# Attention and experts on one core: the low part of the probabilities in tiles of its own, multiplied after the high part

## The chip, the cores and the metric

The kernel runs on one core of one Trainium2 chip. The metric is the device time of one execution in microseconds (us), the median of several runs; lower is better.

## The reference

One transformer block on a sequence of 2048 tokens of width 256, batch 1. Attention has 16 heads of width 128; its weights come as codes times scales of blocks of 32 rows. Then a mixture of 8 experts with hidden width 176, of which each token uses two. Both halves have layer norms before and after, and a residual sum.

```python
q = layernorm(x) @ (wq_codes * repeat(wq_scales, 32)) + bq       # k, v alike
scores = einsum("bqhd,bkhd->bhqk", q, k) / sqrt(128)
attn = softmax(scores, axis=-1)
out = einsum("bhqk,bkhd->bqhd", attn, v).reshape(1, 2048, 2048)
x = x + layernorm(out @ (wo_codes * repeat(wo_scales, 32)) + bo)
y = layernorm(x)
combine = top2_of_softmax(y @ Wr), renormalised, spread over the 8 experts
h = silu(y @ Wg[e]) * (y @ Wu[e])
x = x + layernorm(sum over e of combine[e] * (h @ Wd[e]))
```

Everything is wanted to about float32 precision. TensorE multiplies 16-bit operands here, so the kernel splits each float32 operand into a 16-bit "high part" and the 16-bit rest, the "low part", and adds three products: high by high, high by low, low by high.

## The kernel before, in words

The time goes to attention, from about 30 to 1600 us of the span. Its work is a loop over 256 query tiles of 128 rows (16 tiles for each of 16 heads) plus two passes that only finish (loop variable g; t is the tile's number within the head). Each engine executes its own instructions in the order in which the program emits them: the kernel is written under a manual schedule, so that order is the order of the statements in this loop.

For one query tile:

- `scores_half`, twice: TensorE makes scores of 128 queries by 1024 keys in 6 matmuls of 512 columns (lines 486, 487, 490) in one of three PSUM buffers with the tag "s"; VectorE takes the row maximum (line 491).
- `softmax`: ScalarE takes the exponential of both halves (line 502) into a float32 tile p.
- One tile later: `high_part` (line 516) has ScalarE write the normalised high part ph (float16, three buffers), and SyncE issues a DMA transpose of it (line 519), since the product with the values wants the keys on the partitions. `low_half` (line 531) has VectorE write the low part pl (two buffers) in two halves, the first at the end of that tile, the second at the start of the tile after; behind the second SyncE issues the transpose of pl (line 535).

So SyncE's queue alternates: low part of tile k-2, high part of tile k-1, and so on, 512 transposes in all. Four query tiles make a block. Before the change, both parts of a block's four tiles go to one tile `PT[(h, block)]` of shape 128 x 4 x 32 x 128 (32 KB a partition): in the third dimension 0 to 15 is the high part and 16 to 31 the low part. The pool has two buffers, so the first transpose of block n+2 needs block n's tile to be free: all of its readers must be done.

The product with the values, `pv_part`, works on one block: 16 chunks of 128 keys, three matmuls of 512 columns each, 48 in all, into one PSUM bank ("pv"):

```python
nc.tensor.matmul(ps, vh, d[:, :, c, :], start=(c == 0), stop=False)        # L550
nc.tensor.matmul(ps, vh, d[:, :, 16 + c, :], start=False, stop=False)      # L551
nc.tensor.matmul(ps, vl, d[:, :, c, :], start=False, stop=(c == 15))       # L552
```

vh and vl are the parts of the values, from tiles `V[(pair, group)]` that hold two heads and 512 keys (four a pair of heads, pool tag "v" with seven buffers, which also serves the output weights and tiles of the last stage). The 48 matmuls are cut into 8 units of 6 (`pv_unit`), two units a query tile: unit 2g between the two halves of the scores of tile g and unit 2g+1 behind them. A lag of 13 units (`PVLAG`) puts unit 0 of block n in the second half of tile 4n+6 and unit 7 in the first half of tile 4n+10. The last transpose of block n's high part is issued in tile 4n+4, of its low part in tile 4n+5; the first of block n+2's high part in tile 4n+9.

Between these, `fill` puts the projections of the next Q, K and V (lines 224 and 249), which ScalarE copies out (237, 268) and GpSimd splits; GpSimd also loads and scales weights, and writes each block's attention output to HBM (`ot_d`, line 566).

In the last head, and behind it, the same queues also load the weights of the output projection and of the experts, and reload the attention output in pieces `oi` (`load_oi`, line 682). The last block's units (8 of them, `UEND+1` to `UEND+8`) stand behind the output projection of the first 512 tokens (`op_pass(0, ...)`, line 809), before the router of those tokens (`tr`, `router_a`, `router_b`) and the output projection of the next 512 (`op_mm(1, half, parts)`: a part takes 16 matmuls of 256 columns and reads one piece oi). The expert loop follows (`gate_up`, `down`).

Of the kernel before, what the change touches and what calls it, by code (L numbers as in the profile page):

```python
# [21 lines left out]
D = 256  # L22
# [15 lines left out]
def sandwich(  # L38
# [51 lines left out]
    crow = const.tile([128, D], F32)  # L90
# [4 lines left out]
    def tail_consts(i):  # L95
        if i == 0:
            nc.sync.dma_start(out=crow, in_=bo.partition_broadcast(128))
# [144 lines left out]
    def proj_v(p, t0, n, tag="pj", wide=None):  # L242
# [11 lines left out]
        if t0 % 4 == 0:  # L254
            V[(p, t0 // 4)] = kqv.tile([128, 2, 4, 256], HP, name="v", bufs=7)
# [222 lines left out]
    PT = {}  # L478
# [35 lines left out]
    def high_part(h, t, m, p):  # L514
        ph = soft.tile([128, S], HP, name="ph", bufs=3)
        nc.scalar.activation(ph, p, AF.Copy, scale=m[:, 6:7])  # L516
        if t % 4 == 0:
            PT[(h, t // 4)] = pt.tile([128, 4, 32, 128], HP, name="pt")
        nc.sync.dma_start_transpose(
            out=PT[(h, t // 4)][:, t % 4, 0:16, :], in_=ph  # L520
# [5 lines left out]
    def low_half(half, h, t, m, p, ph):  # L526
# [7 lines left out]
        if half == 1:  # L534
            nc.sync.dma_start_transpose(
                out=PT[(h, t // 4)][:, t % 4, 16:32, :], in_=LOW.pop((h, t))
            )
# [3 lines left out]
    def pv_part(h, b, c0, c1):  # L541
        d = PT[(h, b)]
        if c0 == 0:
            pvps[(h, b)] = psA.tile([128, 512], F32, name="pv")
        ps = pvps[(h, b)]
        dc = bass.ts(h % 2, 128)
        for c in range(c0, c1):
            v = V[(h // 2, c // 4)]
            vh, vl = v[:, 0, c % 4, dc], v[:, 1, c % 4, dc]
            nc.tensor.matmul(ps, vh, d[:, :, c, :], start=(c == 0), stop=False)  # L550
            nc.tensor.matmul(ps, vh, d[:, :, 16 + c, :], start=False, stop=False)  # L551
            nc.tensor.matmul(ps, vl, d[:, :, c, :], start=False, stop=(c == 15))  # L552
        if c1 == 16:
            if (h, b) == (NH - 1, 3):
                o = kqv.tile([128, 2, 512], HP, name="o_last", tag="v", bufs=7)
# [33 lines left out]
    def pv_unit(u):  # L589
        n, e = divmod(u - PVLAG, 8)  # L590
        if 0 <= n < 4 * NH:
            pv_part(n // 4, n % 4, 2 * e, 2 * e + 2)
# [36 lines left out]
    def dequant_wo(j):  # L629
        sc, cd = wo_raw.pop(j)  # L630
        if j % 4 == 0:
            wo.append(kqv.tile([128, 8, D], BF, name="wo", tag="v", bufs=7))
# [45 lines left out]
    def load_oi(b, half, j, tag="kT"):  # L678
        oi = kqv.tile(
            [128, 4, 2, 256], HP, name="oi", tag=tag, bufs={"kT": 8, "v": 7}[tag]  # L680
# [10 lines left out]
    gw = None  # L691
# [5 lines left out]
    def late(t):  # L697
        nonlocal gw
# [159 lines left out]
    def tr(b, kc, tag="pj"):  # L858
        xn = AT[b]
        if kc == 0 and b == 0:  # L860
            XT[b] = [
                kqv.tile([128, 2, 512], F32R, name="xT0", tag="v", bufs=7)
# [14 lines left out]
    def router_a(b, tag="pj"):  # L877
# [9 lines left out]
        if b == 0:  # L887
            LGT[b] = kqv.tile([8, 512], F32, name="lgT0", tag="v", bufs=7)
# [122 lines left out]
    def fin0(b):  # L1011
        y = kqv.tile([128, 4, D], F32, name="y", tag="v", bufs=7)
# [22 lines left out]
    def fin_last(b):  # L1035
        y = kqv.tile([128, 4, D], F32, name="y", tag="v", bufs=7)
# [42 lines left out]
    pv_unit(UEND + 4)  # L1079
    pv_unit(UEND + 5)  # L1080
# [12 lines left out]
    op_mm(1, 0, (0,), "s")  # L1093
# [18 lines left out]
    def load_x1(b):  # L1112
        X1[b] = tl.tile([128, 4, D], F32, name=f"x1_{b}")
# [4 lines left out]
    op_mm(1, 0, (1, 2), "s")  # L1118
# [6 lines left out]
    op_mm(1, 0, (3,), "s")  # L1125
# [99 lines left out]
```

## Time and profile before

| | |
|---|---|
| median of 3 runs | 1871.5 us (1870.53 to 1875.38) |
| the profiled execution | 1870.9 us, of which the span is 1869.1 us |
| TensorE matmul busy | 1785.9 us (96%), 8890 matmuls |
| VectorE busy | 1628.8 us (87%) |
| ScalarE busy | 1366.5 us (73%) |
| GpSimd busy | 937.8 us (50%) |
| DMA: queue 1 (SyncE's, transposes included) | 309.74 MB, 90.4% of 16 engines' span |
| transposes of the high and of the low part | 256 each, median 5.0 us from issue to landing |

How to read it: PE is TensorE's matmuls, PEld its weight loads, which run beside matmuls; DVE is VectorE, ACT ScalarE, POOL GpSimd, SP SyncE. "SPq" is SyncE's queue: the time that it needs to issue a DMA. L551 is line 551. A group is named by what it writes and reads, `pv<-pt,v`; behind "idle before" or in square brackets stands how long the engine was idle ahead of it and what ended that. In a list of waits the three numbers are the sum in us, how often, and the longest. In a timeline a row begins with its start and its length in us.

### The profile page before, as it was taken

To read this page: it belongs to the slowest core of one execution; us is meant where nothing else is said; L and a number is where in the kernel's file an instruction comes from. 1 tells how busy PE (TensorE), PEld (TensorE's weight loads), DVE (VectorE), ACT (ScalarE), POOL (GpSimd) and SP (SyncE) were. 2 spreads that over 40 slices of the span, in tenths; PEclk is the share of its full clock that TensorE was granted. 3 is DMA by queue.
4 is the path that set the end of the run, shared out by engine and by line. 5 is a ranking of instruction groups with operands and counts; after the bars stand their busy time and mean duration, and the time that the engine had idled before them with its cause. 6 is when DMAs were issued, how large, how long until landed. Compare 5 with 4: busy or idle time off the path is not lost. (4 is left out here: it accounts for less than half of the span.)

```text
span 1869.1 us, 25550 instructions
## 1 busy us (share of the span) xinstructions
PE 1785.9 (96%) x8890; PEld 933.7 (50%) x8890; DVE 1628.8 (87%) x2267; ACT 1366.5 (73%) x1730; POOL 937.8 (50%) x929
## 2 busy tenths in 40 slices
PE   7899999999999999999999999999999988999997
PEld 4344444444444444444444444444444334678886
DVE  7999998999898999999999999999999986457566
ACT  5888887888787888888888888887888775123232
POOL 2366565555655565556555656465446442233232
PEclk9999999999999999999999999999999999999999
DMA  2999999999999999999999999999999999982121
GB/s 84 176 199 198 195 200 191 186 199 197 195 186 187 194 197 200 195 197 193 200 197 193 198 199 201 195 192 197 192 187 207 215 221 227 268 222 69 52 75 51
DMA packets 1132529, 342.31 MB, mean 183 GB/s; under 512 B 1071232, under 2 KB 1119568, under 8 KB 1132400
## 3 DMA queue, kind: packets, MB, share of 16 engines
q1 hardware_dynamic: 1119712, 309.74, 90.4%
q0 software_dynamic: 10544, 29.40, 5.7%
q10 hardware_dynamic: 2144, 1.54, 0.3%
q8 instruction: 70, 1.15, 0.2%
q14 instruction: 59, 0.48, 0.1%
HBM read 53.22 MB, written 18.94 MB: 39 GB/s over the span
## 5 line engine op out<-in xcount | busy, mean ns | idle before, releaser
L531 DVE SCALAR_TENSOR_TENSOR pl<-p,m,ph 128x1024 f16<-128x1024 f32 x512 | 723.6, 1414 | 34.5 <-DMA pt<-pl 32.6
L502 ACT ACTIVATE p<-s,m,ssc 128x1024 f32<-128x1024 f32 x512 | 612.3, 1200 | 191.9 <-DVE m L495 175.8
L491 DVE TENSOR_REDUCE m<-s 128x1 f32<-128x1024 f32 x512 | 622.7, 1216 | 43.8 <-PE s L490 41.5
L516 ACT ACTIVATE ph<-p,m 128x2048 f16<-128x2048 f32 x256 | 512.8, 2003 | 79.1 <-ACT t L237 26.7
L551 PE MATMUL pv<-pt,v 128*128 128x512 f16 x1024 | 390.4, 381 | 38.8 <-DMA pt<-pl 38.5
L486 PE MATMUL s<-kT,qT 128*128 128x512 f16 x1024 | 389.7, 381 | 7.3 <-ACT p L502 6.6
L550 PE MATMUL pv<-pt,v 128*128 128x512 f16 x1024 | 390.4, 381 | 3.0 <-DMA pt<-ph 1.7
L552 PE MATMUL pv<-pt,v 128*128 128x512 f16 x1024 | 390.5, 381 | 0.0
L487 PE MATMUL s<-kT,qT 128*128 128x512 f16 x1024 | 389.6, 380 | 0.0
L490 PE MATMUL s<-kT,qT 128*128 128x512 f16 x1024 | 305.5, 380 | 0.0
L238 POOL CAST qT<-t 128x512 f16<-128x512 f32 x63 | 81.8, 1299 | 241.8 <-ACT t L237 241.8
L269 POOL CAST v<-t 128x256 f16<-128x256 f32 (+1 forms) x105 | 45.9, 437 | 285.7 <-ACT t L268 285.7
L551 PEld LDWEIGHTS <-v 128*128 128x128 f16 x1024 | 100.5, 98 | 169.0 <-issue 48.1
L550 PEld LDWEIGHTS <-v 128*128 128x128 f16 x1024 | 100.6, 98 | 126.3 <-issue 4.8
L552 PEld LDWEIGHTS <-v 128*128 128x128 f16 x1024 | 100.6, 98 | 121.7 <-issue 6.1
L490 PEld LDWEIGHTS <-qT 128*128 128x128 f16 x1024 | 100.4, 98 | 121.8 <-issue 1.6
L270 POOL TENSOR_TENSOR v<-t,v 128x256 f16<-128x256 f32 (+1 forms) x105 | 156.9, 1494 | 8.5
L487 PEld LDWEIGHTS <-qT 128*128 128x128 f16 x1024 | 100.5, 98 | 120.3 <-issue 14.5
L486 PEld LDWEIGHTS <-qT 128*128 128x128 f16 x1024 | 100.5, 98 | 110.4 <-issue 1.9
L978 POOL TENSOR_TENSOR hh<-sg,hh 128x512 fp32r<-128x512 f32 x42 | 54.5, 1298 | 143.5 <-ACT hh L977 106.2
L977 ACT CAST hh<-sg 128x512 fp32r<-128x512 f32 (+1 forms) x45 | 27.5, 611 | 117.2 <-DVE sg L989 117.2
L239 POOL TENSOR_TENSOR kT<-t,kT 128x512 f16<-128x512 f32 x60 | 97.7, 1628 | 5.1
(186 smaller groups left out, 2063.4 us busy)
## 6 DMA issues: line engine op xcount, KB each, us to landing
oi<-ot_d SPq DMA_DIRECT2D x32, 512.0 KB, 6.1
ot_d<-o POOLq DMA_DIRECT2D x63, 256.0 KB, 4.4
pt<-ph SPq DMA_TRANSPOSE x256, 5.0
pt<-pl SPq DMA_TRANSPOSE x256, 5.0
cu<-ct_d SPq DMA_DIRECT2D x16, 256.0 KB, 3.7
xt<-in_L_attn_x SPq DMA_DIRECT2D x4, 512.0 KB, 4.6
x<-in_L_attn_x SPq DMA_DIRECT2D x4, 512.0 KB, 6.0
st_s<-in_L_attn_wv_scales POOLq DMA_DIRECT2D x28, 64.0 KB, 4.2
```

The lines of the kernel that those rows point to most:

```text
L239: nc.gpsimd.tensor_tensor(t[:, 1, :], t32, t[:, 0, :], ALU.subtract)
L270: nc.gpsimd.tensor_tensor(v[:, 1, sl, :], t32, v[:, 0, sl, :], ALU.subtract)
L486: nc.tensor.matmul(s[:, j, :], q[:, 0, qc], k[:, 0, :], start=True, stop=False)
L487: nc.tensor.matmul(s[:, j, :], q[:, 0, qc], k[:, 1, :], start=False, stop=False)
L490: nc.tensor.matmul(s[:, j, :], q[:, 1, qc], k[:, 0, :], start=False, stop=True)
L491: nc.vector.tensor_reduce(m[:, half : half + 1], s, AX.XY, ALU.max)
L502: nc.scalar.activation(p[:, bass.ts(i, 1024)], s, AF.Exp, bias=m[:, 2:3], scale=ssc[:, 0:1], accum_out=m[:, 3 + i : 4 + i],)
L516: nc.scalar.activation(ph, p, AF.Copy, scale=m[:, 6:7])
L531: nc.vector.scalar_tensor_tensor(pl[:, cs], p[:, cs], m[:, 6:7], ph[:, cs], ALU.mult, ALU.subtract)
L550: nc.tensor.matmul(ps, vh, d[:, :, c, :], start=(c == 0), stop=False)
L551: nc.tensor.matmul(ps, vh, d[:, :, 16 + c, :], start=False, stop=False)
L552: nc.tensor.matmul(ps, vl, d[:, :, c, :], start=False, stop=(c == 15))
```

## The change

- The transposed parts get tiles of their own: `pth` for the high part and `ptl` for the low part, each 128 x 4 x 16 x 128 with two buffers (the same memory in all).
- The 48 products of a block are reordered: first, chunk by chunk, high probabilities by high and by low values (32 matmuls), then high values by low probabilities (16). Cut into 8 units of 6 as before: units 0 to 4 and a third of unit 5 read `pth`, the rest reads `ptl`.
- The tag "v" has eight buffers instead of seven. To make room, `crow` (the output bias row) is loaded in the last head instead of the first, into memory that is free by then, and the residual tile `x1_1` takes a buffer with the tag "v".
- Behind the loop, parts 0 and 1 of `op_mm(1, 0)` move ahead of the last block's unit 4; parts 2 and 3 follow at the places shown.

```diff
-            PT[(h, t // 4)] = pt.tile([128, 4, 32, 128], HP, name="pt")
+            PT[(h, t // 4)] = pt.tile([128, 4, 16, 128], HP, name="pth")
         nc.sync.dma_start_transpose(
-            out=PT[(h, t // 4)][:, t % 4, 0:16, :], in_=ph
+            out=PT[(h, t // 4)][:, t % 4], in_=ph
         )
...
         if half == 1:
+            if t % 4 == 0:
+                PTL[(h, t // 4)] = pt.tile([128, 4, 16, 128], HP, name="ptl")
             nc.sync.dma_start_transpose(
-                out=PT[(h, t // 4)][:, t % 4, 16:32, :], in_=LOW.pop((h, t))
+                out=PTL[(h, t // 4)][:, t % 4], in_=LOW.pop((h, t))
             )
...
+    PV_ORDER = [(c, i) for c in range(16) for i in (0, 1)]
+    PV_ORDER += [(c, 2) for c in range(16)]
+
-    def pv_part(h, b, c0, c1):
-        d = PT[(h, b)]
-        if c0 == 0:
+    def pv_part(h, b, e):
+        if e == 0:
             pvps[(h, b)] = psA.tile([128, 512], F32, name="pv")
...
-        for c in range(c0, c1):
-            v = V[(h // 2, c // 4)]
-            vh, vl = v[:, 0, c % 4, dc], v[:, 1, c % 4, dc]
-            nc.tensor.matmul(ps, vh, d[:, :, c, :], start=(c == 0), stop=False)
-            nc.tensor.matmul(ps, vh, d[:, :, 16 + c, :], start=False, stop=False)
-            nc.tensor.matmul(ps, vl, d[:, :, c, :], start=False, stop=(c == 15))
-        if c1 == 16:
+        for n in range(6 * e, 6 * e + 6):
+            c, i = PV_ORDER[n]
+            d = (PTL if i == 2 else PT)[(h, b)]
+            nc.tensor.matmul(
+                ps, V[(h // 2, c // 4)][:, i % 2, c % 4, dc], d[:, :, c, :],
+                start=(n == 0), stop=(n == 47),
+            )
+        if e == 7:
...
             gw = rp.tile([128, 2, 2, EI], F32R)
+            crow = rp.tile([128, D], F32)
+            nc.sync.dma_start(out=crow, in_=bo.partition_broadcast(128))
...
     pv_unit(UEND + 4)
+    op_mm(1, 0, (0, 1), "s")
     pv_unit(UEND + 5)
...
     router_a(0, "s")
-    op_mm(1, 0, (0,), "s")
+    op_mm(1, 0, (2,), "s")
     router_b(0, "s")
...
+        if b == 1:
+            X1[b] = kqv.tile([128, 4, D], F32, name="x1_1", tag="v", bufs=8)
+        else:
+            X1[b] = tl.tile([128, 4, D], F32, name=f"x1_{b}")
...
-    op_mm(1, 0, (1, 2), "s")
+    op_mm(1, 0, (3,), "s")
     router_d(0)
...
-    op_mm(1, 0, (3,), "s")
```

More of the change, by code (lines that the diff above doesn't have):

```diff
@@ L89, in sandwich @@
     bv3 = const.tile([128, NH, 3], BF)
-    crow = const.tile([128, D], F32)
     rst = const.tile([128, 2, E], F32)
@@ L96, in tail_consts @@
         if i == 0:
-            nc.sync.dma_start(out=crow, in_=bo.partition_broadcast(128))
             nc.sync.dma_start(out=rst, in_=wr.rearrange("(kc p) e -> p kc e", p=128))
@@ L254, in proj_v @@
         if t0 % 4 == 0:
-            V[(p, t0 // 4)] = kqv.tile([128, 2, 4, 256], HP, name="v", bufs=7)
+            V[(p, t0 // 4)] = kqv.tile([128, 2, 4, 256], HP, name="v", bufs=8)
         v = V[(p, t0 // 4)]
@@ L475, in sandwich @@
     soft = soft_ctx.enter_context(tc.tile_pool(name="soft", bufs=2, reuse_waits="tile"))
-    PT = {}
+    PT, PTL = {}, {}
     def scores_half(h, t, half, m):
@@ L546, in pv_part @@
         dc = bass.ts(h % 2, 128)
-        for c in range(c0, c1):
-            v = V[(h // 2, c // 4)]
-            vh, vl = v[:, 0, c % 4, dc], v[:, 1, c % 4, dc]
-            nc.tensor.matmul(ps, vh, d[:, :, c, :], start=(c == 0), stop=False)
-            nc.tensor.matmul(ps, vh, d[:, :, 16 + c, :], start=False, stop=False)
-            nc.tensor.matmul(ps, vl, d[:, :, c, :], start=False, stop=(c == 15))
-        if c1 == 16:
+        for n in range(6 * e, 6 * e + 6):
[6 more added lines that the diff above has]
+        if e == 7:
             if (h, b) == (NH - 1, 3):
-                o = kqv.tile([128, 2, 512], HP, name="o_last", tag="v", bufs=7)
+                o = kqv.tile([128, 2, 512], HP, name="o_last", tag="v", bufs=8)
                 nc.scalar.activation(o[:, 0, :], ps, AF.Copy, scale=1.0 / PS)
@@ L591, in pv_unit @@
         if 0 <= n < 4 * NH:
-            pv_part(n // 4, n % 4, 2 * e, 2 * e + 2)
+            pv_part(n // 4, n % 4, e)
     wo = []
@@ L631, in dequant_wo @@
         if j % 4 == 0:
-            wo.append(kqv.tile([128, 8, D], BF, name="wo", tag="v", bufs=7))
+            wo.append(kqv.tile([128, 8, D], BF, name="wo", tag="v", bufs=8))
         hs = slice(2 * (j % 4), 2 * (j % 4) + 2)
@@ L679, in load_oi @@
         oi = kqv.tile(
-            [128, 4, 2, 256], HP, name="oi", tag=tag, bufs={"kT": 8, "v": 7}[tag]
+            [128, 4, 2, 256], HP, name="oi", tag=tag, bufs={"kT": 8, "v": 8}[tag]
         )
@@ L690, in sandwich @@
     prev = None
-    gw = None
+    gw, crow = None, None
     gst = {}
@@ L697, in late @@
     def late(t):
-        nonlocal gw
+        nonlocal gw, crow
         if t in WO_LOAD:
@@ L861, in tr @@
             XT[b] = [
-                kqv.tile([128, 2, 512], F32R, name="xT0", tag="v", bufs=7)
+                kqv.tile([128, 2, 512], F32R, name="xT0", tag="v", bufs=8)
                 for _ in range(2)
@@ L887, in router_a @@
         if b == 0:
-            LGT[b] = kqv.tile([8, 512], F32, name="lgT0", tag="v", bufs=7)
+            LGT[b] = kqv.tile([8, 512], F32, name="lgT0", tag="v", bufs=8)
         else:
@@ L1011, in fin0 @@
     def fin0(b):
-        y = kqv.tile([128, 4, D], F32, name="y", tag="v", bufs=7)
+        y = kqv.tile([128, 4, D], F32, name="y", tag="v", bufs=8)
         nc.scalar.copy(y, DPS.pop(b)[1])
@@ L1035, in fin_last @@
     def fin_last(b):
-        y = kqv.tile([128, 4, D], F32, name="y", tag="v", bufs=7)
+        y = kqv.tile([128, 4, D], F32, name="y", tag="v", bufs=8)
         mv = small.tile([128, 4, 2], F32, name="mv3")
@@ L1112, in load_x1 @@
     def load_x1(b):
-        X1[b] = tl.tile([128, 4, D], F32, name=f"x1_{b}")
+        if b == 1:
+            X1[b] = kqv.tile([128, 4, D], F32, name="x1_1", tag="v", bufs=8)
+        else:
+            X1[b] = tl.tile([128, 4, D], F32, name=f"x1_{b}")
         nc.sync.dma_start(out=X1[b], in_=XV[:, b])
```

## The prediction, made before the changed kernel ran

> **What bounds the kernel now.** I read the busy times first, then TensorE's waits by stage, then single blocks in the order of time, then the waits of the engines around them. All idle times below are of heads 1 to 14 (127 to 1467 us from the start) unless said otherwise.
>
> The stages (columns: stretch, length, then busy us and count of PE, PEld, DVE, ACT, POOL, then granted clock, DMA share, GB/s):
>
> ```profile
> 127.00:1467.00 1340.00, 1314.10 (x6258) 610.55 (x6256) 1251.99 (x1568) 1118.84 (x1390) 761.90 (x765) 1.00 1.08 196
> 1467.00:1600.00 133.00, 114.97 (x576) 56.51 (x574) 98.79 (x132) 85.08 (x101) 42.16 (x34) 0.96 1.12 225
> 1600.00:1642.00 42.00, 38.52 (x245) 27.63 (x245) 22.71 (x61) 9.65 (x15) 16.06 (x11) 0.96 1.04 279
> ```
>
> TensorE has 26 us of idle time in 1340, VectorE 88, and the DMA engines are never free on average. TensorE's waits in heads 1 to 14, then those of head 15 and after:
>
> ```profile
> PE pv L551 <- DMA pt<-pl: 23.3, 22, 2.6
> PE s L486 <- ACT p L502: 1.6, 2, 1.2
> ...
> PE pv L551 <- DMA pt<-pl: 14.2, 5, 4.2
> PE s L486 <- ACT p L502: 4.1, 3, 3.0
> PE pv L550 <- DMA pt<-ph: 1.7, 2, 1.2
> ```
>
> One wait is nearly all: line 551, the product with the low part, for the transpose of that low part. In one block:
>
> ```profile
> 889.04 0.38 PE L550 MATMUL pv<-pt,v 128*128 128x512 f16 x1
> ...
> 890.63 0.38 PE L551 MATMUL pv<-pt,v 128*128 128x512 f16 x1 [1.21 <-DMA pt<-pl]
> 890.84 0.38 PE L552 MATMUL pv<-pt,v 128*128 128x512 f16 x1
> ```
>
> The high product starts; the second instruction of the block stands 1.21 us. In a stream, starts lie 0.215 apart (0.21 to 0.22 by these lines) but each is shown 0.38 long, so a listed wait is about 0.165 too short: 23.3 + 22 x 0.165 = 26.9 us.
>
> From the starts of the first score matmul of each query tile I worked out the tile times of heads 1 to 14: nearly all are 6.04 (a tile with a Q or K projection) or 5.62 us (with a V projection), which is TensorE's own work: 24 matmuls x 0.2155 = 5.17, plus 4 x 0.2155 or 4 x 0.109. A head of such tiles is 93.3 us (91.5 for head 14); the real mean is (1467.4 - 127.1) / 14 = 95.7. The excess is 36.2 us over 14 heads, and 31.6 of it lies in tiles 2, 6, 10 and 14, the ones in whose second half a block of products begins; 3.1 in the tile after, mostly half-clock matmuls behind a long wait. So TensorE sets the pace, and it loses 34.7 us where a block begins.
>
> Why the low part is late: SyncE issues all transposes, and the first one of block n+2 waits for the last product of block n, which frees the shared tile.
>
> ```profile
> SPq L519 <- PE pv L552: 45.5, 41, 2.4
> ...
> DVE m L491 <- PE s L490: 32.6, 58, 2.5
> ...
> DVE pl L531 <- DMA pt<-pl: 13.8, 18, 1.8
> ```
>
> SyncE loses 45.5 us there (about 1.1 per hold), and its 447 transposes last 1214.7 us by their own durations (2.72 each), so it is over 90% taken and doesn't catch up quickly.
>
> **The Trainium skill.** "TensorE: Matmul & The Clock Gate", section "Back-to-back issue gap", gives N / 2.4 + 2.5 ns, 215.8 for 512 columns: the trace agrees (0.215 to 0.216). The same page, "What's actually happening", says that the array falls to half clock after an idle window of about 3.4 us: the trace agrees, behind the waits of 4.15 and 3.85 us at 1569 and 1602 matmuls start 0.43 apart for some us. "DMA: Bandwidth & Descriptors", "Anatomy of one DMA", says that a semaphore wait is served on the issuing sequencer before dispatch, so one held transpose holds all behind it: the 45.5 us above agree. The same page, "Issuing engines are not separate DMA queues", says that all issuers share 16 engines: the DMA share of 1.08 agrees.
>
> **The change, part by part.**
> Same work: still 48 matmuls and 48 weight loads a block. Weights now alternate high, low for 32 of them; each load takes 98 ns with or without a new weight before (lines 550 to 552 all show 98) under a 215 ns matmul: nothing. If that cover went, 48 x 98 ns a block, but no row shows a bare load. The 4 KB instead of 8 KB stride between query tiles of the moving operand is not shown by any row; I take 0 and keep 1 us a head as its bound either way.
>
> *First low product.* It moves from unit 0 to unit 5 of a block, 2.5 tiles (14.6 us) later. The worst wait is 4.2, so all of them go in the loop: 34.7 us with the half-clock share. High parts are still due at unit 0. The last one of a block is issued just ahead of the third low one and lands 5.0 us later: in the block shown issued at 882.48, due at 889.04, 1.5 us spare, in the block 72 us earlier 3.9. No wait of line 550 stands in heads 1 to 14. But what SyncE lacks over several blocks is no longer made good by waits for low parts, so I take 2 us of waits for high parts (bounds 0 and 12).
>
> *The held transpose.* High tiles are read in units 0 to 5 only, so the buffer is free one tile before its next transpose is issued; the hold of 45.5 us ends. The new hold, of the first low transpose of a block, is for unit 7 of block n: TensorE runs that within 1.3 us after the tile's first scores, while VectorE needs a 1.22 reduce, two small steps and a 1.4 low step after the same scores. The wait is over before the transpose is ready: 0. Behind it on SyncE would stand the next high transpose.
>
> *What is late next.* VectorE. Its idle time is 88.0, 32.6 of it for TensorE's scores; the rest, 55.4, is for ScalarE, for buffers of low parts and small gaps. A loop shorter by 34.7 leaves it 53.3, less than the 55.4. So it becomes an equal of TensorE, and the waits don't fall together: I take back a quarter, 9 us (bounds 2 and 25), as TensorE waiting at line 486 for score buffers. Loop: -34.7 + 2 + 9 = -23.7.
>
> *Head 15.* From 1451 to 1601 SyncE is taken without a break (62 DMAs, 142.7 us of issue in 150, no gap over 0.43): transposes with loads of weights and attention outputs between them. No held transpose is among them, so this stretch keeps its length, whatever TensorE gains. crow's load moves into it from head 0, where it cost nothing and saves nothing: one more issue, +0.5 by the neighbours (0.53).
>
> *Behind the last transpose:*
>
> ```profile
> 1596.32 3.64 SPq L535 DMA_TRANSPOSE pt<-pl  x1
> 1597.81 0.39 PE L550 MATMUL pv<-pt,v 128*128 128x512 f16 x1 [0.57 <-DMA pt<-ph]
> 1601.23 5.10 SPq L682 DMA_DIRECT2D oi<-ot_d  x4
> 1602.05 0.61 PE L551 MATMUL pv<-pt,v 128*128 128x512 f16 x1 [3.85 <-DMA pt<-pl]
> ```
>
> Now four units of high products run at once (4 x 1.29, to 1603.0), then 32 output matmuls (3.5), then the low ones. But those 32 read loads that SyncE issues at 1601.2 and 1601.8, behind the last transpose; the second lands at 1608.5. So 4.0 of wait and 1.7 of half clock (3.4 us at half) are exchanged for about 4 of another wait; the gain is some 2 us (bounds: a loss of 4, a gain of 6). The pass now holds one of three score buffers from there on; two are left to the two transposes and the router, which need each other's results anyway: 0.
>
> *Eight value buffers.* Low-part products read all four value tiles to the end of a pair's last block; with eight, no tile of the next pair needs one of them. 0. x1_1 in such a buffer waits for the last product; its load is issued at 1618 anyway: 0.
>
> Sum: -23.7 + 0.5 - 2 = -25.2. The profiled execution took 1870.9 (span 1869.1): 1845.7. The median of the runs is 1871.5, 0.6 higher: 1846.3, rounded 1846.
>
> **Rivals.**
> *Full gain.* VectorE keeps up. For it: in most tiles TensorE finds a free score buffer 0.7 to 3 us ahead. -34.7 - 6 (tail's best) + 0.5: 1831.
> *The transposes are the bound.* For it: DMA share 1.08, SyncE over 90% taken; where it issues back to back without a break for ten or more, I find about 3.0 us from one to the next, so 6.0 a tile, which is the present 5.98. Against it: back to back over all, it is 2.90, or 5.80 a tile, below TensorE's 5.83, and tiles at TensorE's floor are the rule. Gain only 0 to 5: 1869, at the present pace of 2.99.
> *Slower: transposes collide.* Held transposes leave the DMA engines free now and then; without the holds each is issued onto the one before, beside weight loads and output stores. If that takes all of them to 3.03, just above the mean of those long runs (3.00; from 2.93 to 3.12), a tile is 6.06 against 5.98: 0.08 x 224 tiles of heads 1 to 14 = 18, so 1889. It decides from 2.99 on, the present mean. Against it: the long runs are those in which transposes were slow for another reason, and the bytes are the same.
> High parts late at unit 0 are how the second rival would show on TensorE.
>
> **How the numbers follow.** Forecast 1846 (1836 to 1857): 0.61. Full gain 1831: 0.17. Transposes 1869: 0.15. Collision 1889: 0.07. Range 1830 to 1868: it takes in most of the first two and the better end of the third. About 0.3% (5.6 us) is what a measurement can tell. Faster by over that 0.82 (the first two and 0.04 of the third), same 0.11, slower 0.07.
>
> **What would show it.** Right: TensorE's wait for pt<-pl under 3 us in the loop; SyncE's wait for PE gone; VectorE's wait for scores down from 32.6 to near 10; some 5 to 15 us of TensorE at the scores, for ScalarE. Head 15 as long as before; a wait of 3 to 5 us ahead of the moved output matmuls. Wrong: transposes back to back through the loop with tiles of 6 us, or TensorE waiting for high parts at the start of blocks.

## The result and the profile after

The changed kernel takes 1862.3 us (median of 8 runs, 1859.3 to 1866.4), the kernel before in the same session 1872.0 (8 runs, 1868.6 to 1876.0): a ratio of 0.995, interval 0.9935 to 0.9964, so 9.7 us less. The forecast was 1846.3, 25.2 less than the 1871.5 known then. The sign and the kind of gain are right, the size is not: 16 us are missing. Of all runs in this document one, of e11 at 1872.8 us, was in a slower state of the chip and is not counted.

First the stages of the changed kernel (columns as in the first fence of the prediction): heads 1 to 14, head 15 up to the issue of the last transpose, and all that comes behind it, the tail.

```profile
126.30:1448.60 1322.30, 1311.26 (x6258) 611.69 (x6256) 1252.32 (x1569) 1118.01 (x1391) 766.36 (x765) 1.00 1.09 198
1448.60:1580.40 131.80, 116.76 (x573) 56.77 (x571) 94.09 (x121) 85.35 (x101) 41.19 (x34) 0.95 1.11 222
1580.40:1860.30 279.90, 258.50 (x1576) 216.26 (x1576) 172.08 (x396) 71.12 (x123) 81.33 (x63) 0.96 0.42 116
```

With the same marks read from the trace before (head 1 at 127.1, head 15 at 1467.4, last transpose at 1596.3, end at 1869.1) the stages compare so, in us:

| stage | before | after | difference | forecast |
|---|---|---|---|---|
| head 0 | 127.1 | 126.3 | -0.8 | 0 |
| heads 1 to 14 | 1340.3 | 1322.3 | -18.0 | -23.7 |
| head 15 to the last transpose | 128.9 | 131.8 | +2.9 | +0.5 |
| tail | 272.8 | 279.9 | +7.1 | -2 |
| sum | 1869.1 | 1860.3 | -8.8 | -25.2 |

Most of what was hoped for came in the loop. Then more than a third of it was given back in the tail, where a small gain was expected. These are single traces. A second one of the changed kernel (e15, below) has 126.3, 1318.4, 133.7 and 280.6 us: the loop and head 15 vary by 2 to 4 us from trace to trace, the tail by less than 1. Of the kernel before there is one trace only.

**The loop.** The waits of TensorE and VectorE in heads 1 to 14 of the changed kernel (engine, result and line, what was waited for, us in all, times, longest):

```profile
PE pv L552 <- POOL v L268: 4.7, 7, 0.8
PE s L484 <- ACT p L500: 4.3, 7, 1.9
PE pv L552 <- POOL v L267: 1.0, 1, 1.0
...
DVE m L507 <- ACT p L500: 18.5, 68, 0.4
DVE m L489 <- PE s L488: 17.1, 32, 2.9
DVE pl L529 <- DMA ptl<-pl: 7.8, 9, 1.8
```

The 23.3 us for low parts are gone, none of the waits is for a high part, and SyncE's wait for the last product (45.5 us) no longer stands in its list. VectorE's wait for scores has fallen from 32.6 to 17.1 (forecast: near 10). TensorE now waits for score buffers (4.3, forecast 5 to 15), and for something that was not forecast: GpSimd's low part of the values. The place is tile 8 of even heads. GpSimd and TensorE around that tile in head 10, where it cost most:

```profile
1025.12 1.56 POOL L267 CAST v<-t 128x512 f16<-128x512 f32 x1 [5.64 <-ACT t L266]
1026.76 1.15 POOL L268 TENSOR_TENSOR v<-t,v 128x512 f16<-128x512 f32 x1
```

```profile
1026.74 0.39 PE L552 MATMUL pv<-pth,v 128*128 128x512 f16 x1 [0.97 <-POOL v L267]
1027.97 0.39 PE L552 MATMUL pv<-pth,v 128*128 128x512 f16 x1 [0.84 <-POOL v L268]
```

GpSimd ends the high half at 1026.7 and the low half at 1027.9, and each time a product starts at once. The value tiles 14 and 15 are projected in tile 7. Before, their products lay in the last of eight units of a block; in the new order all products with high probabilities are done in units 0 to 5, so these two tiles are needed 14 and 15 products, some two and a half units, earlier. From the starts of the first score matmul, a tile in which TensorE never waits (its floor) takes 6.04 us here; tile 8 of heads 2, 4, ... 14 takes 6.82 to 8.87, and in head 10 the next tile runs at half clock for a while (matmuls of 512 columns start 0.43 us apart instead of 0.215, and the tile takes 7.28 instead of 5.62). Of the loop's excess over TensorE's floor, 36.2 before and 18.3 now, 9.4 lie in these tiles and 8.9 elsewhere, mostly where TensorE finds no free score buffer. In e15's trace of the same kernel it is 5.7 and 8.6.

**The tail.** TensorE from its first output products to the first gate and up products:

```profile
1562.04 8.90 PE L814 MATMUL op_s<-wo,oi 128*128 128x256 bf16 x80
1573.30 5.50 PE L814 MATMUL op_s<-wo,oi 128*128 128x256 bf16 x48 [2.36 <-DMA oi<-ot_d]
1581.69 7.04 PE L552 MATMUL pv<-pth,v 128*128 128x512 f16 x24 [2.90 <-DMA pth<-ph]
1590.84 3.73 PE L814 MATMUL op_s<-wo,oi 128*128 128x256 bf16 x32 [2.11 <-DMA oi<-ot_d]
...
1598.39 0.30 PE L876 MATMUL trp_s<-ident,at 128*128 128x128 f32 x1
1599.98 1.41 PE L876 MATMUL trp_s<-ident,at 128*128 128x128 f32 x7 [1.28 <-DVE at L841]
...
1615.79 1.63 PE L969 MATMUL gup<-xT,gw 128*128 128x512 f32 x6
```

The high products of the last block run before its last transpose, issued at 1580.4, has landed, and the moved 32 output products wait for their loads, both as forecast. New is what VectorE does meanwhile. It finishes its last low part at 1570.3 and should add up the residual (at) when the output products of 1562 and 1573 are done, near 1571 and 1579:

```profile
1567.78 2.48 DVE L529 SCALAR_TENSOR_TENSOR pl<-p,m,ph 128x1024 f16<-128x1024 f32 x2 [3.53 <-DMA ptl<-pl]
1586.03 0.75 DVE L823 SCALAR_TENSOR_TENSOR at<-op_s,sig,crow 128x512 f32<-128x512 f32 x1 [15.78 <-DMA ptl<-pl]
```

It stands 15.8 us, until the last low part's transpose has landed, though at reads nothing of it. Before, the same line waited for the output products alone:

```profile
1590.29 0.75 DVE L818 SCALAR_TENSOR_TENSOR at<-op_s,sig,crow 128x512 f32<-128x512 f32 x1 [2.48 <-PE op_s L809]
1597.28 0.75 DVE L818 SCALAR_TENSOR_TENSOR at<-op_s,sig,crow 128x512 f32<-128x512 f32 x1 [5.23 <-PE op_s L809]
```

And behind the tail's start ScalarE comes late to the experts: its first sigmoid (L989) stands behind casts of the down weights, which wait for their loads.

```profile
1615.62 1.05 ACT L656 CAST dw<-draw 128x1024 fp32r<-128x1024 f32 x1 [5.96 <-DMA draw<-in_L_ffn_Wd]
1621.32 1.05 ACT L656 CAST dw<-draw 128x1024 fp32r<-128x1024 f32 x1 [4.66 <-DMA draw<-in_L_ffn_Wd]
1622.28 0.59 ACT L989 ACTIVATE sg<-gup 128x512 f32<-128x512 f32 x1
```

The first gate products start at 1615.8, the first sigmoid 6.5 us later; before it was 3.2 (1630.6 and 1633.8). TensorE then waits at the first down and the fourth gate products (passes of gate and up are counted from 0, so the fourth is pass 3), and runs them at half clock: six gate products take 2.93 us there, otherwise about 1.6.

### The profile page after: what moved, and what is told of

Its sections match the earlier page's. It is cut to its first block, busy times and chain, and to the rows that moved or that the text cites. A ratio compares the mean times of both kernels' runs of the same rounds, so it can differ in the third digit from the quotient of the medians.

```text
span 1860.3 us, 25554 instructions
## 1 busy us (share of the span) xinstructions
PE 1789.9 (96%) x8890; PEld 937.8 (50%) x8890; DVE 1627.9 (88%) x2267; ACT 1365.3 (73%) x1730; POOL 941.2 (51%) x929
## 5 line engine op out<-in xcount | busy, mean ns | idle before, releaser
L529 DVE SCALAR_TENSOR_TENSOR pl<-p,m,ph 128x1024 f16<-128x1024 f32 x512 | 723.4, 1413 | 32.6 <-DMA ptl<-pl 27.9
L552 PE MATMUL pv<-pth,v 128*128 128x512 f16 x2048 | 508.1, 381 | 9.7 <-POOL v L268 4.7
L552 PE MATMUL pv<-ptl,v 128*128 128x512 f16 x1024 | 253.2, 380 | 0.0
L236 POOL CAST qT<-t 128x512 f16<-128x512 f32 x63 | 76.4, 1212 | 239.0 <-ACT t L235 239.0
L500 ACT ACTIVATION_READ_ACCUMULATOR p<-s,m,ssc 128x1 f32 x512 | 99.0, 193 | 0.0
L568 POOL TENSOR_TENSOR o<-t,o 128x512 f16<-128x512 f32 x63 | 96.2, 1527 | 5.2
L236 POOL CAST kT<-t 128x512 f16<-128x512 f32 x60 | 65.6, 1094 | 64.1 <-ACT t L235 64.1
L237 POOL TENSOR_TENSOR kT<-t,kT 128x512 f16<-128x512 f32 x60 | 88.0, 1467 | 5.1
```

The lines of the kernel that those rows point to most:

```text
L236: nc.gpsimd.tensor_copy(t[:, 0, :], t32)
L500: nc.scalar.activation(p[:, bass.ts(i, 1024)], s, AF.Exp, bias=m[:, 2:3], scale=ssc[:, 0:1], accum_out=m[:, 3 + i : 4 + i],)
L529: nc.vector.scalar_tensor_tensor(pl[:, cs], p[:, cs], m[:, 6:7], ph[:, cs], ALU.mult, ALU.subtract)
L552: nc.tensor.matmul(ps, V[(h // 2, c // 4)][:, i % 2, c % 4, dc], d[:, :, c, :], start=(n == 0), stop=(n == 47),)
L568: nc.gpsimd.tensor_tensor(o[:, 1, :], t32, o[:, 0, :], ALU.subtract)
```

## The experiments

Theory: the reorder gains in the loop what it takes from the low-part waits, minus a new wait for values and the score buffers; the tail loses by side effects of the same change, its moved products and its memory. Rival: the transposes, or the buffers' freeing of SyncE, set the loop, and the tail is late as a matter of course. The experiments ran in five groups, each on one chip: e1 to e4, e5 to e8, e9 to e12, e13 and e14, e15 to e18. Ratios are to the kernel before on the same chip; one interval is about 0.2% (4 us) to either side, so stage lengths from the profiles, one trace of each kernel, are used for smaller parts.

### Which part made the gain of the loop: e1 and e12

e1 keeps one shared tile of both parts; the new order and the rest of the change stay:

```
-            PT[(h, t // 4)] = pt.tile([128, 4, 16, 128], HP, name="pth")
+            PT[(h, t // 4)] = pt.tile([128, 4, 32, 128], HP, name="pt")
...
-            d = (PTL if i == 2 else PT)[(h, b)]
+            d = PT[(h, b)][:, :, 16:32, :] if i == 2 else PT[(h, b)][:, :, 0:16, :]
```

> Everything of the change except the split: both parts share one tile again, so the first transpose of block n+2 is held by SyncE until unit 7 of block n. Late low parts are what TensorE waits for (my theory): the new order alone ends TensorE's wait for pt<-pl in heads 1 to 14 (23.3 us listed before, under 2 now), the hold of SyncE for TensorE stays at 30 to 45 us, and the time is within 3 us of the changed kernel, 1860 to 1865. Rival, the hold is what makes transposes late: TensorE then waits at unit 0 for high parts instead, 15 us or more, and the time is 1868 to 1872.

Measured: 1867.0, ratio 0.9963 (0.9944 to 0.9983), 2 us above the range of the theory; the loop takes 1326.7, 13.5 less than before. SyncE is still held by the products (40.0 us, 40 times), and TensorE has no wait for a part, so the theory of the waits holds and the rival does not.

e12 keeps the separate tiles, and the rest of the change, and puts back the old order:

```
-    PV_ORDER = [(c, i) for c in range(16) for i in (0, 1)]
-    PV_ORDER += [(c, 2) for c in range(16)]
+    PV_ORDER = [(c, i) for c in range(16) for i in (0, 2, 1)]
```

> The changed kernel with the products in the order of before (high with high, high with low, low with high, block by block of keys), so that the two buffers for each part, the eighth value buffer, crow and the moved output products are all that is left of the change. Theory (the gain of the loop is the order; the buffers alone only free SyncE, which the order makes worth 2 to 4 us): PE waits 28 us or more for low parts in heads 1 to 14, the loop takes 1336 to 1342 us as before, and the time is 1869 to 1877, so not faster than before. Rival (freeing SyncE from PE brings the transposes early enough by itself): the loop falls below 1330 and the time below 1865.

Measured: 1875.2, ratio 1.0013 (1.0001 to 1.0025), not faster than before. Its waits in heads 1 to 14, TensorE's and then SyncE's:

```profile
PE pv L551 <- DMA ptl<-pl: 15.0, 20, 2.2
PE s L484 <- ACT p L500: 2.0, 3, 1.2
...
SPq L517 <- PE pv L551: 47.1, 45, 2.0
```

The low parts are waited for again, and SyncE is held as long as ever, now by the high tile, since in the old order both tiles are read to a block's end. The loop still takes 1330.1, 10.2 less than before, so my numbers for it (1336 to 1342, and 28 us of waits) are misses, and why the loop gains that with the hold in place I did not find. It is not shown that the separate tiles bring it, since e12 also keeps the eighth value buffer and the new addresses. Head 15 and the tail give it all back (133.6 against 128.9, and 281.9 against 272.8). The loop gains 13.5 with the order and no split, 10.2 with the split and no order, and 18.0 (21.9 in e15's trace) with both; whether the two parts add up can't be told from traces that vary by 4 us. Without the order the change is worth nothing.

### What is late next in the loop: e3, e7, e8, e9, e10

e3 projects the late value tiles of even heads earlier:

```
-            if t in (3, 5) and h > 0:
-                proj_v(p, 12 + (t - 3) // 2, 1, wide=soft)
-            elif t == 7 and h > 0:
-                proj_v(p, 14, 2, wide=soft)
+            if t == 3 and h > 0:
+                proj_v(p, 12, 2, wide=soft)
+            elif t in (5, 7) and h > 0:
+                proj_v(p, 14 + (t - 5) // 2, 1, wide=soft)
```

> The changed kernel with value tiles 12 and 13 of a pair both projected in query tile 3, 14 in tile 5 and 15 in tile 7 (before: 12 in 3, 13 in 5, 14 and 15 in 7). If TensorE's new wait for GpSimd's low part of the values in tile 8 of even heads is the price of multiplying by those values two units earlier, it goes (7 waits, 5.7 us listed, 7 with the modelled ends, 1.7 to 3.4 more of half clock), and the time is 1853 to 1857. Rival, the time reappears as waits for score buffers: 1860 to 1863.

Measured: 1860.7, ratio 0.9919 (0.9896 to 0.9942). Tile 8 of even heads is back at 6.04 us and the wait for values is gone, yet the loop takes 1321.6, as in the changed kernel, and the time is the rival's: the only wait that TensorE has left in it grew from 4.3 to 7.8 us, and VectorE's for a low-part buffer from 7.8 to 17.9.

```profile
DVE pl L529 <- DMA ptl<-pl: 17.9, 19, 3.7
PE s L484 <- ACT p L500: 7.8, 11, 3.4
```

e7 goes back to seven value buffers (in every place that names them) and to x1_1 in the tail's pool:

```
-            V[(p, t0 // 4)] = kqv.tile([128, 2, 4, 256], HP, name="v", bufs=8)
+            V[(p, t0 // 4)] = kqv.tile([128, 2, 4, 256], HP, name="v", bufs=7)
...
-            X1[b] = kqv.tile([128, 4, D], F32, name="x1_1", tag="v", bufs=8)
+            X1[b] = tl.tile([128, 4, D], F32, name=f"x1_{b}")
```

e8 adds to that a third buffer for low parts, in the 4 KB that became free, with the tiles' order of e5 below:

```
-            LOW[(h, t)] = soft.tile([128, S], HP, name="pl")
+            LOW[(h, t)] = soft.tile([128, S], HP, name="pl", bufs=3)
```

> The changed kernel with seven value buffers as before, and the residual rows of block 1 in the tail's own pool as before; everything above the value buffers lies 4 KB lower, so that at and pl do not overlap. Theory (the eighth buffer brings nothing to the loop and costs the overlap): heads 1 to 14 within 3 us of the changed kernel's 1322, VectorE's wait at the at line gone, 1857 to 1861. Rival (the eighth buffer carries the gain, because projected values wait for a buffer without it): PE or GpSimd waits at the value projections show, the loop is over 1330 us and the time over 1866.

Measured: 1857.2, ratio 0.9916 (0.9896 to 0.9936); the loop 1320.7. The eighth buffer brings nothing to the loop in the new order.

> Seven value buffers as in the run beside it, and the 4 KB given to a third buffer for low parts (pl). Theory (VectorE is held by low parts whose transposes have not landed, 9 to 18 us in the loop, and so frees the score buffers late, for which PE waits 8 to 11 us): VectorE's wait for ptl<-pl falls under 3 us, PE's waits for score buffers halve, and the time is 3 to 7 us under the run with seven value buffers. Rival (VectorE's or ScalarE's own work sets the score buffers): the wait for pl goes, PE's waits stay at 7 to 11 us, and the time is within 2 us of the run beside it.

Measured: 1849.1, ratio 0.9877 (0.9859 to 0.9896), the loop 1311.9. The waits of e8's TensorE and VectorE:

```profile
PE pv L555 <- POOL v L268: 3.4, 7, 0.8
PE s L487 <- ACT p L503: 0.5, 2, 0.3
...
DVE m L492 <- PE s L491: 18.0, 38, 1.6
DVE pl L532 <- issue: 2.2, 14, 0.2
```

VectorE no longer waits for a low-part buffer, and TensorE's waits for score buffers fall with that to 0.5 us. So those waits, which the prediction put down to VectorE's own work, came from VectorE standing still for a buffer whose transpose had not landed.

e9 and e10 go on from there: e9 also puts the output products of block 1 back at their old places (as e2 below, except that part 3 is written behind the two casts of down weights instead of ahead of them; these casts are ScalarE's and GpSimd's work), e10 adds the edit of e3.

> Seven value buffers and a third pl buffer, as in e8, and the output products of block 1 at their places of before. Theory (moving these products ahead of the first transposes of the tail leaves PE waiting for their loads and takes away what covered the start of the experts; that is independent of the loop): 5 to 8 us under e8, 1841 to 1845, with the experts' first block as in the kernel before (gate_up pass 5 begins 28 to 29.5 us after pass 0). Rival (with the loop shorter the tail hangs on something else, so the two gains don't add): within 3 us of e8, 1846 to 1851.

Measured: 1846.0, ratio 0.9869 (0.9843 to 0.9896). The tail is 8.1 us shorter than e8's (272.9 against 281.1), as the theory has it, but the medians differ by 3.1 only and the time is the rival's, so by the times this gain is not shown. The profiled spans differ by 11.0, for the profiled run of e8 took 1854.2, the most of its five, and that of e9 1843.2, nearly the least of its five. From pass 0 of gate and up to pass 5 it is 33.1 us instead of the 28 to 29.5 that I expected; 6.5 of the 8.1 us are won ahead of pass 0.

> As e9, and in even heads the value tiles 12 and 13 are projected in tile 3, 14 in tile 5 and 15 in tile 7, so that GpSimd's split of the last values has more time before the products of tile 8 need it. Theory A (values and score buffers are two limits behind each other: without the third pl buffer the 7 us saved on values came back as waits for score buffers): PE's wait for GpSimd's v goes and heads 1 to 14 shorten by 4 to 7 us against e9; 1836 to 1840. Theory B (the wait for values costs nothing of its own, PE loses the same time elsewhere): within 2 us of e9.

Measured: 1841.9, ratio 0.9842 (0.9818 to 0.9866): the fastest kernel of the study, 1.6% under the one before. That is 4.1 under e9, though 2 us above the range of theory A. The loop takes 1308.4, 4.1 less than e9's, with a floor of 1304.1. The other traces agree: 1311.9 to 1312.6 without this edit (e8, e9, e11), 1308.4 and 1308.6 with it (e10, e14). So values and score buffers are two limits, one behind the other: taking away the first alone (e3) gained nothing, after the second it gains 4.

### Where the tail lost: e2, e4, e5, e6 and a square of four

e2 puts the output products of block 1 back at their old places:

```
     pv_unit(UEND + 4)
-    op_mm(1, 0, (0, 1), "s")
...
     router_a(0, "s")
-    op_mm(1, 0, (2,), "s")
+    op_mm(1, 0, (0,), "s")
...
-    op_mm(1, 0, (3,), "s")
+    op_mm(1, 0, (1, 2), "s")
     router_d(0)
...
+    op_mm(1, 0, (3,), "s")
     split_d(*d0)
```

> The changed kernel with the parts of the output projection of the second 512 tokens back at their old places behind the last block. If the moved parts cost (TensorE stands 2.1 and 0.5 us at them for loads of attention output, and the router's work starts behind them), the last products end 4 to 6 us earlier and the time is 1858 to 1861. If they cover a wait for the last low part, TensorE waits 3 to 5 us at unit 5 or at the router, and the time is 1863 to 1867.

Measured: 1859.3, ratio 0.9913 (0.9888 to 0.9939). The experts run as before (238.0 us from the first gate product to the end, before 238.5, in the changed kernel 244.6), but the tail is only 1.9 shorter, for now TensorE waits at the first transposes of the tail for at, 8.7 us. So the time fits the forecast but not its reason: counted from the last transpose, the last products end 1.7 us later, not 4 to 6 earlier.

e4 defers the second cast of down weights by one pass, so that ScalarE's sigmoid is not behind it:

```
-    split_d(*d1)
...
-        1: [lambda: ln_b2(1)],
+        1: [lambda: ln_b2(1), lambda: split_d(*d1)],
```

> The changed kernel with the second cast of the down weights (split_d) behind the second gate-up pass of the first token block instead of ahead of all of them. If ScalarE's first sigmoid stands behind a cast that waits for a load (4.7 us, in the profile of the changed kernel), TensorE's idle time and half clock after the first three gate-up passes (some 5 us) go: 1856 to 1859. Rival, the router's combine weights come just as late: 1861 to 1863.

Measured: 1861.5, ratio 0.9922 (0.9898 to 0.9946). The sigmoid comes 3.0 us behind the first gate product, and pass 3 10.4 instead of 15.4; then TensorE waits 6.4 us at pass 4 for the routing weights (cu), whose loads stand on SyncE behind eight loads of heads. From the first gate product to the end it is 244.5, as without the edit, and the time is the rival's. The late sigmoid was a symptom.

The addresses of the tiles in the built programs gave the other suspect. Before, the first at buffer begins at byte 198624 of a partition and the second pl buffer ends at 196576. In the changed kernel crow, moved to the other end of memory, pushes at down by 1 KB to 197600, and the eighth value buffer less crow pushes pl up by 3 KB, to end at 199648. They share 2 KB, so at may be written only after the last transpose has read pl. e5 allocates the softmax's tiles in another order, with the temporary t32 behind pl, which then ends at 195552:

```
     soft = soft_ctx.enter_context(tc.tile_pool(name="soft", bufs=2, reuse_waits="tile"))
+    for name, dtype, bufs in (("p", F32, 2), ("ph", HP, 3), ("pl", HP, 2)):
+        for _ in range(bufs):
+            soft.tile([128, S], dtype, name=name, bufs=bufs)
```

> The changed kernel with one difference: in the pool of the softmax the temporary t32 is placed behind the two buffers for low parts (pl) and no longer ahead of the high parts, so that the first at buffer of the tail no longer shares 2 KB per partition with the second pl buffer, which the eighth value buffer had pushed up by 4 KB. Theory (the first residual of the tail waits for the landing of the last low-part transpose only because of that shared memory): VectorE's wait of 15.8 us at the at line falls below 8 us and is put down to the output products; the transposes of the first block (PE trp) wait for nothing; the time falls by 2 to 5 us against the changed kernel, to 1857 to 1860, because PE itself waited only 1.7 us there and the rest is what its late chain costs at the start of the experts. Rival (the wait is that of the loads of heads and low parts anyway, memory plays no part): the wait stays at 14 to 16 us and the time at 1861 to 1864.

Measured: 1861.5, ratio 0.9942 (0.9921 to 0.9963). VectorE's wait for the transpose at the at line is gone, and the two halves of the residual are added at 1572.1 and 1580.7; what VectorE still waits there is 1.4 and 6.8 us, the longer one for the output products, and together about the 8 that I expected. The time is not different, as the rival has it; the tail is 1.6 shorter. e6 has the edits of e2 and e5:

> The kernel with the output products of block 1 at their places of before, and with the pl and at buffers apart as in the run beside it. Theory: with the filler gone, PE waited 8.7 us for the first residual (at) in the run without the second edit; with the memory apart this goes, so 1849 to 1854, and the stretch from the last transpose to the end is 270 to 274 us instead of 278. Rival (the chain is late for another reason): 1858 to 1861, with PE still waiting 7 us at trp.

Measured: 1854.5, ratio 0.9911 (0.9889 to 0.9932), tail 270.7. By the ratio it is no better than e2, by the tail 7.3 us. So all four corners were run together: e15 is the changed kernel, e16 has the edit of e5, e17 that of e2, e18 both.

> The changed kernel itself: moved output products, and at sharing 2 KB with pl. One corner of a square of four kernels on one chip. Theory (each of the two costs the tail some us, and each hides part of the other): 1861 to 1864 by the earlier runs. Rival (only the moved products cost anything; the shared memory is a wait beside the path): the same here, it parts at the last corner.

> Second corner: moved output products, memory apart (the edit of e5). Theory: 1 to 3 us under the first corner, with tail (issue of the last transpose to the end) 278 to 280 us. Rival: within 1 us of the first corner.

> Third corner: output products at their old places, memory shared (the edit of e2). Theory: 3 to 5 us under the first corner, tail 276 to 279 us, PE waiting 7 us or more at trp for at. Rival: 6 to 8 us under it, as far as the last corner.

> Fourth corner: old places and memory apart (the edits of e6). Theory: 3 to 7 us under the third corner, tail 270 to 273 us, PE's wait at trp under 2 us. Rival: within 1.5 us of the third corner.

Measured (tails in us from the profiled executions; in brackets those of the changed kernel, e5, e2 and e6, which are the same four kernels):

| | memory shared | memory apart |
|---|---|---|
| products moved | e15: 1860.8, 0.9944 (0.9924 to 0.9964), tail 280.6 (279.9) | e16: 1861.7, 0.9941 (0.9921 to 0.9961), tail 278.3 (278.3) |
| products at old places | e17: 1859.3, 0.9940 (0.9918 to 0.9962), tail 278.3 (278.0) | e18: 1855.8, 0.9927 (0.9902 to 0.9953), tail 271.2 (270.7) |

The intervals of the four times overlap, so the times alone settle nothing, and two of them miss the theory: e16 is no faster than e15, and e17 is 1.5 us faster, not 3 to 5. From the first to the last corner the medians fall by 5.0 us and the tails by 9.4; where the rest is, one trace of each cannot tell. The tails repeat within 0.7 us between the sessions, and they are clear: 280, 278, 278, 271. Each of the two alone costs 7 us, both together 9, so undoing one shows little.

The two costs lie in different places. From the last transpose's issue to the first gate product e15 to e18 take 36.3, 34.8, 40.9 and 32.4 us, from there to pass 7 of gate and up 51.3, 50.4, 44.4 and 45.8, and from pass 7 to the end 193.0 in all four. So with the products at their old places the shared memory costs 8.5 us, all of it ahead of the experts; with the products moved TensorE has work during that wait, and comes late to the transposes of at in any case. The moved products are paid for mostly behind the first gate product (4.6 us with the memory apart, 6.9 with it shared).

In e17, with the memory shared, VectorE's at and TensorE's transposes of it:

```profile
1581.08 0.75 DVE L823 SCALAR_TENSOR_TENSOR at<-op_s,sig,crow 128x512 f32<-128x512 f32 x1 [15.73 <-DMA ptl<-pl]
...
1593.43 0.45 PE L876 MATMUL trp_s<-ident,at 128*128 128x128 f32 x1 [7.48 <-DVE at L841]
1595.02 1.97 PE L876 MATMUL trp_s<-ident,at 128*128 128x128 f32 x7 [1.14 <-DVE at L841]
```

In e18, with the memory apart:

```profile
1570.88 0.75 DVE L826 SCALAR_TENSOR_TENSOR at<-op_s,sig,crow 128x512 f32<-128x512 f32 x1 [1.42 <-DMA ot_d<-o]
1580.92 0.75 DVE L826 SCALAR_TENSOR_TENSOR at<-op_s,sig,crow 128x512 f32<-128x512 f32 x1 [8.28 <-PE op_s L817]
...
1591.64 0.30 PE L879 MATMUL trp_s<-ident,at 128*128 128x128 f32 x1 [1.51 <-DVE at L844]
1593.22 1.41 PE L879 MATMUL trp_s<-ident,at 128*128 128x128 f32 x7 [1.28 <-DVE at L844]
```

The wait for the transpose has become one for the output products, and the transposes of at follow the products of the block closely (2.8 us of waits, where I expected under 2). With the products moved (e16) that doesn't help, since TensorE itself comes to these transposes late, behind the products that wait for their loads.

### Head 15: e11, e13, e14

e11 is e9 with 18 loads of head 15 issued by GpSimd (nc.gpsimd in place of nc.sync for five loads of wo codes, four of gate weights, crow and the eight pieces oi of block 0).

> As e9, and the 18 ordinary loads that SyncE issues between the transposes of head 15 (wo codes, gate weights, crow, heads of block 0; 13 us of its queue) are issued by GpSimd. Theory (head 15 is bound by what SyncE issues one after the other): head 15, from its first scores to the issue of the last transpose, shortens from 132 to 119-125 us, and the time falls by 6 to 12 us against e9. Rival (head 15 is bound by the transfers themselves, not by who issues them): the transposes' own issue time grows from 110 us by what the loads leave, and the time is within 3 us of e9.

Measured: 1855.6 (median of five), ratio 0.9899 (0.9865 to 0.9933), 9.6 over e9, and spread more widely than any other kernel (1843 to 1860). Head 15 takes 149.3 us instead of 131.2. Both expectations are wrong, and in the same direction, although of the rival's signs one came: the transposes' own issue time grew, by far more than the loads had taken (13 us). SyncE's transposes in e11 while GpSimd issues:

```profile
1511.41 1.94 SPq L538 DMA_TRANSPOSE ptl<-pl  x1
1513.44 5.62 SPq L520 DMA_TRANSPOSE pth<-ph  x1
1519.17 11.26 SPq L538 DMA_TRANSPOSE ptl<-pl  x1
1530.52 11.78 SPq L520 DMA_TRANSPOSE pth<-ph  x1
```

The 36 transposes of the head occupy SyncE for 142 us instead of 110. "DMA: Bandwidth & Descriptors" of the Trainium skill, section "Issuing engines are not separate DMA queues", says that issuing from several engines saves only the sequencer's time; that nothing is gained agrees, that it costs 18 us is not in it, and here the measurement decides.

e13 is the changed kernel with crow loaded in head 0 again, e14 the same edit on e10:

```
+    crow = const.tile([128, D], F32)
...
-            crow = rp.tile([128, D], F32)
-            nc.sync.dma_start(out=crow, in_=bo.partition_broadcast(128))
```

> The changed kernel with crow back in the constants and loaded in head 0, as before the change; at and pl still share 2 KB. Theory (the load of crow between two transposes of head 15 is what makes the head longer: 0.87 us of its own and the next low-part transposes' issue at 6.5 us instead of 5.2): head 15, first scores to the issue of the last transpose, takes 128 to 130 us as before instead of 132 to 134, and the time falls by 2 to 4 us against the changed kernel, to 1858 to 1860. Rival (the head runs from 129 to 134 us in whatever kernel, as its transposes and loads happen to meet, and crow is 0.9 of it): 131 to 134 us, and 1861 to 1863.5.

> The fastest version so far (third pl buffer, seven value buffers, output products of block 1 at their old places, late value tiles projected earlier) with crow loaded in head 0. Theory: the same 2 to 4 us, so 1838 to 1840. Rival: within 1.5 us of the version without this edit, 1840.5 to 1843.5.

Measured: e13 1869.4, ratio 0.9985 (0.9973 to 0.9997), head 15 135.4; e14 1843.5, ratio 0.9845 (0.9821 to 0.9868), head 15 131.5 against e10's 131.7. The load of crow is not what makes the head longer. That e13 is slower than the changed kernel was expected by nobody; in the traces its loop is 3.5 us and its head 15 another 3.6 longer (7.4 and 1.7 against e15), and its tiles lie 1 KB higher. I did not find the cause.

## Why the prediction was wrong, by its own steps

*First low product: right.* All waits for low parts went, and high parts cost nothing instead of 2 us. *The held transpose: right that the hold ends.* It takes both parts of the change: with the old order it stayed at 47.1 us (e12), with one shared tile at 40.0 (e1). Set against e1, freeing SyncE is worth 4.4 us of the loop, or 8.3 with e15's trace; in the times it is 5.5 (e1 against e4, which has the changed loop and ran on the same chip).

*What is late next: the size about right, the reason wrong, and one term missing.* Score buffers and all else cost 8.9 us (8.6 in e15), forecast 9. But the limit was not VectorE's work: with a third low-part buffer TensorE's waits for score buffers fall to 0.5 us (e8). The missing term belongs under *Eight value buffers*, which was put at 0. The prediction asked whether there are enough buffers for values; it did not ask when the last value tile is ready. The new order reads it two and a half units earlier, and the loop pays for it at tile 8, 9.4 us in one trace and 5.7 in the other. The loop lacks 5.7 us in the first; the term can't simply be set against that, since without it the score buffers cost more (e3). The profiled loops of the kernels with the changed loop and memory within a few KB of it (the changed one, e2, e4, e5, e6, e15 to e18) range from 1317.8 to 1323.7, so the shortfall is 1 to 7 us.

*Head 15: +0.5 forecast, +2.9 measured, cause open.* crow was cleared by e13 and e14. Apart from e11, the other kernels show 131 to 135 us there; only the one trace of before shows 128.9, and how far that one would vary is not known.

*Behind the last transpose: the failed step.* A gain of 2 us was forecast, a loss of 7.1 measured. "The gain is some 2 us" was worked out for this block of products alone. With the two side effects undone the tail is 271.2 and 270.7 (e18, e6), 1.5 and 2.1 us under the 272.8 of before; but e9, e10 and e14, which also have both undone and a third low-part buffer beside, show 272.8 to 274.0, so this small gain is not certain. What the step left out cost 9 us. First, the moved output products were priced by their own wait alone (about 4 us; measured 2.1 in the changed kernel, 3.6 in e5). They were also the work that had covered the chain from the transposes of at over the router to the casts of the down weights and the routing weights. Put ahead of that chain, they cover nothing behind it: from the last wait of the transposes of at (trp) to the first gate product the changed kernel has 15.8 us, e18 18.7, so the gate products come sooner than what they need, and TensorE stands and runs at half clock among them. Second, crow's move and the eighth value buffer were costed as a load and as a buffer, +0.5 and 0. They also move the tiles allocated above them, and so at got memory whose earlier user, the second pl buffer, is free only when the last transpose has read it.

*The rivals.* The transposes are not the bound: e10 runs the loop within 4.3 us of TensorE's floor with the same transposes, as heads 3 and 7 of the changed kernel already did (5.83 a tile). No collision of transposes shows in the loop either. That the range of 1830 to 1868 held the 1862.3 was luck: its upper end was drawn for the rival of the transposes, which the runs speak against, while the forecast's own range ended at 1857 and the tail lost 7.1 us where its bound was a loss of 4.

*The clock and the spacing of matmuls.* The prediction finds that its trace agrees with "TensorE: Matmul & The Clock Gate" of the Trainium skill, section "What's actually happening", on half clock after an idle window of about 3.4 us. It agrees at the two waits named there; but in the same trace single waits of 2.06 and 2.10 us, which end at 313.6 and 579.5, are also followed by matmuls 0.43 us apart, about 1 us after they end, and so are, in head 10 of the changed kernel, two waits of 0.97 and 0.84 us with one product between them. So a wait under 3.4 us can cost half clock too. The 215.8 ns for 512 columns, from the section "Back-to-back issue gap" of the same page, are given there for an isolated matmul, and about 131 ns for a sustained stream; the streams here show 0.215 us, and the measurement decides.

## What to carry to other kernels

A change of a buffer's count or pool also moves the tiles allocated above it: compare the addresses of the two built programs, and ask of each tile of the next stage whose memory it inherits and when that owner's last reader is done. Work that is moved forward to fill a wait leaves the place where it was, so name what it covered there; and when a reordered loop needs its operands earlier, check the producer of every operand, not only the one whose lateness was the reason. If undoing one suspect shows little, undo both: here two causes of 7 us each in the tail showed 2 when one was undone, and in the loop the wait for score buffers hid that for values.

## What the runs showed of the hardware that was not expected

Ordinary loads issued by GpSimd beside SyncE's stream of DMA transposes made single transposes occupy SyncE for up to 11.8 us, against 1.3 to 6.5 in that stretch of the kernels before and after, where the loads are in SyncE's own queue; the stretch grew from 131 (e9) to 149 us (e11). Which of the loads does it, and whether another engine's queue would do the same, was not tried.
